# Seven large work tiles, five gate tiles, three cells and two attention tiles in the second stage of a four-layer graph network

## The chip, the cores and the metric

The kernel runs on one core of one Trainium2 chip. The metric is the device time of one execution in microseconds (us), lower is better, given as the median of several runs of the same program.

The core has a matrix engine (TensorE, "PE" in the profile, with its weight loads listed apart as "PEld"), a vector engine (VectorE, "DVE"), an activation engine (ScalarE, "ACT"), a general one (GpSimd, "POOL") and one that issues DMAs here (SyncE, "SP"). Each has its own instruction queue and works it off in order; they meet at semaphores. Matrix products land in PSUM, a memory of eight banks. Everything else lives in SBUF, 128 partitions wide.

## What is computed

The input `x` has 128 samples of 64 nodes with 256 features, and `adj` is one 64x64 adjacency matrix. Four layers follow each other, each with a residual sum and a layer norm:

```
x = layernorm(x + L0(x, adj))   # three graph convolutions, 256 -> 512 -> 1024 -> 256
x = layernorm(x + L1(x, adj))   # U relu(U^T x W1 + b1) W2 + b2, U the eigenvectors of the Laplacian
x = layernorm(x + L2(x, adj))   # two graph convolutions, then windowed LSTMs
x = layernorm(x + L3(x, adj))   # attention of the nodes, masked by adj
```

The LSTM part of L2 is the heavy one. For p = 1, 2, 3, 4 the nodes are cut into windows of p in a row, a small LSTM with its own weights runs over each window, and its last state replaces the last node of the window:

```
for p in range(1, 5):
    wins = h[:, :nw * p, :].reshape(Bv * nw, p, Hd)
    last = _lstm_last(Wih[p - 1], Whh[p - 1], bih[p - 1], bhh[p - 1], wins)
    h = h.at[:, idx, :].set(last.reshape(Bv, nw, Hd))
```

so the LSTM of p+1 reads what that of p wrote, and each LSTM step needs the state of the step before.

## The kernel before

The 8192 rows (128 samples x 64 nodes) are 64 tiles of 128 rows, worked on in 16 groups of 4 tiles. All arithmetic is float32.

**First stage** (lines up to about 1120, 0 to about 795 us): layer 0 for all groups, with the eigenvectors of the Laplacian worked out in between on DVE. Its matmuls are issued in `mm` (line 940). It isn't touched by the change.

**Second stage** (from about 797 us to the end): layers 1 to 3. `unit` (line 1518) describes the work of one unit. Groups 0 to 11 go in six units of two groups, groups 12 to 15 in four units of one. For each group a unit calls `layer1`, then `to_lstm` (the two graph convolutions, then `lstm` for p = 1, 2, 3); then for the pair together `four` (the LSTM of p = 4, whose later steps go through `halves`, a product scheme with fewer multiplications that needs sums of the weights, "sums"); then for each group `from_lstm` (back to rows, residual sum, norm) and `layer3` (attention, residual sum, norm, output DMA). The text calls the passage in which a unit runs `from_lstm` and `layer3` a changeover, because by then another unit has to supply the LSTM matmuls.

`norm` (line 1232) is a chain across engines: DVE takes statistics, POOL adds a constant and raises to the power -1/2, DVE (or ACT in the last groups) scales the rows `X`. Matmuls that read the new `X` wait for that chain.

The order of the instructions isn't written by hand. A planner, `Plan` (lines 104 to 233), first notes each operation with an estimated length and its dependencies (`note`), then emits them one by one (`run`). It keeps up to `UNITS` = 3 units open at a time. At each pick it takes, for each engine, the operations that are ready, works out when each could begin by its own estimates, and emits the earliest, an operation of an older group first where they tie. All its instructions pass through `emit`, so the profile shows them all under line 156.

Buffers enter the planner as counted slots. An operation that opens a new tile can begin only once a slot of that kind is free; if all are held, it is no candidate and something else is taken. A slot comes free when the last operation that touches its tile is done. The kinds are:

| kind | what it holds | size per partition | slots before | name, line |
|---|---|---|---|---|
| `w` | large work tiles: results of `mixed`, the LSTM input and output `hT`, the differences in `halves`, `xT`, `hT` and `hn` of `layer3` | 4 KB | 6 | `WIDE`, 742 |
| `gates` | the gates of one half of an LSTM step | 4 KB | 6 | `GATES`, 743 |
| `att` | exponentials of the scores in `layer3` | 2 KB | 3 | `ATT`, 744 |
| `c` | LSTM cell states | 2 KB | 4 | `CELLS`, 745 |
| `hs` | LSTM outputs between steps | 2 KB | 4 | `OUTS`, 746 |
| `v` | small work tiles | 2 KB | 4 | in the call of `Plan` |
| `ps` | PSUM banks | | 8 | in the call of `Plan` |

The `hT` of a group is a `w` tile that is opened in `to_lstm` and held until `from_lstm` has read it. An `lstm` step opens two `gates` tiles; an LSTM with p > 1 opens one cell tile for all its steps. The four names reach the planner in one call:

```
plan = Plan({...}, place,
            {"ps": 8, "w": WIDE, "v": 4, "gates": GATES, "c": CELLS, "hs": OUTS, "att": ATT, ...})
```

`ATT` is also the length of the loop that allocates the attention tiles and clears each of them with a memset on POOL (line 1149). While more than three groups are left, a guard in `candidates` also keeps younger units from taking the last free slots of a kind: it leaves the oldest unit as many as `MOST` says, 4 of `w`, 2 of `v`, `ps` banks 4, 2 of `gates`, 2 of `hs`, and one of each other kind, less those that the oldest unit holds already.

Of the kernel before, what the change touches and what calls it, by code (L numbers as in the profile page):

```python
# [738 lines left out]
EPS = 1e-5  # L739
UNITS = 3  # L740
ENDING = (14, 15)
WIDE = 6
GATES = 6
ATT = 3
CELLS = 4
OUTS = 4
LASTS = 3
SINGLE = 4
# [59 lines left out]
def kernel(  # L808
# [337 lines left out]
    att = []  # L1146
    for i in range(ATT):
        att.append(wb.tile([P, 4, P], F32, name=f"att{i}"))
# [3 lines left out]
    def place(tag, slot, shape):  # L1152
# [4 lines left out]
        if tag in ("w", "v", "gates", "c", "hs"):  # L1157
# [3 lines left out]
    plan = Plan({"PE": nc.tensor, "DVE": nc.vector, "ACT": nc.scalar, "POOL": nc.gpsimd, "SP": nc.sync}, place,  # L1161
                {"ps": 8, "w": WIDE, "v": 4, "gates": GATES, "c": CELLS, "hs": OUTS, "att": ATT, "mx": 4, "sm": 4, "st": 4, "mv": 4,
                 "rs": 4, "nm": 4})
# [434 lines left out]
```

## Time and profile before

| | |
|---|---|
| median of 3 runs | 2471.87 us (2471.45 to 2472.79) |
| the profiled execution's own time | 2474.36 us |
| its span, first to last instruction | 2472.6 us |
| mean granted clock of PE | 0.996 |
| PE busy | 2438.2 us (99%), 15500 matmul records |
| DVE busy | 1618.9 us (65%) |
| ACT busy | 1072.3 us (43%) |
| POOL busy | 137.4 us (6%) |

Engine times are sums over the span. Each float32 matmul of the program leaves two matmul records, a transpose one. A row of the profile reads: line, engine, operation, the tile written, an arrow, the tiles read, shapes, count. In a list of waits, "PE ps <- DVE X" means that PE was about to write a `ps` tile and was released by the DVE instruction that wrote `X`. In a table of stretches each row is one stretch of the span: its limits and length, the busy time of each engine with its instruction count, then the share of full clock that PE was granted, the share of the DMA engines and their rate in GB/s.

### The profile page before, as it was taken

The numbers are of one execution on the slowest core, as the hardware profiler recorded it, in microseconds if no ns is written. First come the engines' busy times: TensorE is split into PE (matmuls) and PEld (weight loads), VectorE is DVE, ScalarE is ACT, GpSimd is POOL, SyncE is SP. The second block draws the span as 40 slices with busy tenths as digits, with TensorE's granted clock in tenths as the row PEclk, the third lists the DMA queues.
The fourth block names the chain that finished last, engine by engine and source line by source line (L and its number), as shares of the span: only waits on it lengthen the run. The fifth ranks groups of instructions, "written<-read, shape, count | busy, mean of one in ns | idle before, by whom it ended". The sixth has DMA issues, their size and how long they took to land.

```text
span 2472.6 us, 40811 instructions
## 1 busy us (share of the span) xinstructions
PE 2438.2 (99%) x15500; PEld 2162.5 (87%) x15500; DVE 1618.9 (65%) x5676; ACT 1072.3 (43%) x2610; POOL 137.4 (6%) x316
## 2 busy tenths in 40 slices
PE   9999999999999999999999999999999999999997
PEld 7788888878887899989978999999998997988996
DVE  6888787778887274583674476476458468374336
ACT  2343343333333354444434444444444444445555
POOL 0000000000000010010010000000001001010002
PEclk9999999999999999999999999999999999999999
DMA  6000000000000110010000001001001000000000
GB/s 225 9 1 18 10 9 10 9 10 9 10 1 1 64 56 1 1 35 1 1 18 18 1 1 35 1 1 35 1 1 35 1 1 18 1 10 1 1 1 27
DMA packets 27973, 42.69 MB, mean 17 GB/s; under 512 B 2945, under 2 KB 22145, under 8 KB 27777
## 3 DMA queue, kind: packets, MB, share of 16 engines
q1 hardware_dynamic: 27424, 39.81, 4.6%
q8 instruction: 122, 2.00, 0.3%
q14 instruction: 75, 0.61, 0.1%
q10 hardware_dynamic: 352, 0.28, 0.0%
HBM read 26.45 MB, written 13.63 MB: 16 GB/s over the span
## 4 chain that ended last, share of the span: by engine, by line
PE 93%; DVE 5%; POOL 1%; DMA 1%; ACT 0%; issue 0%; SPq 0%; ACTq 0%; POOLq 0%; DVEq 0%
PE ps L156 61%; PE ps L940 31%; DVE X L156 1%; DVE D L52 1%; DVE st L156 1%; PE pc L296 1%; DMA XA<-in_x_dram 1%; DVE gates L156 0%; POOL rs L156 0%; DVE tw L52 0%; DVE w L156 0%; ACT gates L156 0%; DVE h L52 0%; DVE u L52 0%; DVE mv L156 0%
## 5 line engine op out<-in xcount | busy, mean ns | idle before, releaser
L156 PE MATMUL ps<-w,wih 128*128 128x168 f32 (+2 forms) x4144 | 753.7, 315 | 0.9 <-DVE gates L156 0.9
L156 PEld LDWEIGHTS ps<-w,wih 128*128 128x128 f32 x4144 | 647.6, 191 | 38.1 <-issue 6.9
L156 ACT ACTIVATE gates<-ps,cbi 128x168 f32<-128x168 f32 (+2 forms) x832 | 342.8, 418 | 368.5 <-PE ps L156 360.3
L156 PE MATMUL ps<-hs,whh 128*128 128x168 f32 (+1 forms) x1952 | 344.8, 291 | 0.0
L156 PEld LDWEIGHTS ps<-hs,whh 128*128 128x128 f32 x1952 | 289.2, 191 | 1.7 <-issue 1.4
L156 PE MATMUL ps<-w,sums 128*128 128x128 f32 x1776 | 237.1, 275 | 0.0
L156 DVE SCALAR_TENSOR_TENSOR gates<-gates 128x256 f32<-128x256 f32 (+2 forms) x220 | 84.0, 382 | 222.8 <-ACT gates L156 222.2
L940 PE MATMUL ps<-aw,h 128*128 128x256 f32 x1024 | 227.2, 379 | 0.0
L156 PEld LDWEIGHTS ps<-w,sums 128*128 128x128 f32 x1776 | 217.5, 192 | 0.6 <-issue 0.5
L940 PEld LDWEIGHTS ps<-aw,h 128*128 128x128 f32 x1024 | 192.9, 190 | 25.9 <-ACT h L949 0.5
L156 ACT ACTIVATE gates<-gates,cbi 128x256 f32<-128x256 f32 x272 | 116.4, 497 | 206.6 <-DVE gates L156 206.5
L949 ACT ACTIVATE h<-h 128x512 f32<-128x512 f32 x128 | 80.5, 630 | 196.6 <-DVE h L52 196.5
L156 DVE TENSOR_TENSOR gates<-gates,ps 128x256 f32<-128x256 f32 x340 | 128.7, 417 | 21.3 <-PE ps L156 15.9
L940 PE MATMUL ps<-ss,tw 128*128 128x256 f32 x512 | 117.9, 380 | 0.0
L940 PE MATMUL ps<-ss,aw 128*128 128x256 f32 x512 | 117.3, 379 | 0.0
L940 PE MATMUL ps<-m,aw 128*128 128x256 f32 x512 | 117.1, 380 | 0.0
L156 DVE SCALAR_TENSOR_TENSOR c<-gates,c 128x256 f32<-128x256 f32 (+2 forms) x156 | 57.2, 367 | 88.6 <-ACT gates L156 88.2
L940 PE MATMUL ps<-aw,m 128*128 128x512 f32 x256 | 114.8, 594 | 0.1
L940 PEld LDWEIGHTS ps<-ss,aw 128*128 128x128 f32 x512 | 96.6, 190 | 12.8
L940 PEld LDWEIGHTS ps<-ss,tw 128*128 128x128 f32 x512 | 96.3, 190 | 12.9 <-issue 0.2
L156 DVE TENSOR_TENSOR gates<-v,ps 128x256 f32<-128x256 f32 x136 | 55.5, 417 | 79.5 <-ACT v L156 47.7
L940 PEld LDWEIGHTS ps<-m,aw 128*128 128x128 f32 x512 | 95.6, 190 | 12.6 <-issue 0.5
(314 smaller groups left out, 3743.0 us busy)
## 6 DMA issues: line engine op xcount, KB each, us to landing
out_dram<-X SPq DMA_DIRECT2D x64, 128.0 KB, 1.7
rest<-XA SPq DMA_DIRECT2D x10, 512.0 KB, 2.6
X<-rest SPq DMA_DIRECT2D x10, 512.0 KB, 3.2
XA<-in_x_dram SPq DMA_DIRECT2D x18, 256.0 KB, 6.2
wih<-in_c_ih_dram SPq DMA_DIRECT2D x4, 1024.0 KB, 7.4
aw<-in_a_w_dram SPq DMA_DIRECT2D x3, 1024.0 KB, 10.8
X<-in_x_dram SPq DMA_DIRECT2D x12, 256.0 KB, 5.9
whh<-in_c_hh_dram SPq DMA_DIRECT2D x3, 1024.0 KB, 9.3
```

Of the source, the lines that this page charges most:

```text
L52: return getattr(self.engine, name)(out, *args, **kw)
L156: getattr(e, name)(*[real(x) for x in args], **{k: real(v) for k, v in kw.items()})
L296: PE.matmul(out, lhsT, rhs, start=True, stop=True)
L940: PE.matmul(out, lhsT, rhs, start=start, stop=stop)
L949: S.activation(dst, src, AF.Relu)
```

## The change

Four constants take other values. Nothing else in the file differs.

```diff
-WIDE = 6
-GATES = 6
-ATT = 3
-CELLS = 4
+WIDE = 7
+GATES = 5
+ATT = 2
+CELLS = 3
 OUTS = 4
 LASTS = 3
```

The tiles of these four kinds take 7 x 4 + 5 x 4 + 2 x 2 + 3 x 2 = 58 KB of each partition instead of 6 x 4 + 6 x 4 + 3 x 2 + 4 x 2 = 62 KB. The planner gets other slot counts, so it may emit the second stage in another order; one memset of an attention tile falls away.

## The prediction

> **What bounds the kernel now.** I read the page first, then stretches of the second stage by busy time of each engine, then the waits of the tensor engine in the worst stretch, then the chain that ended last and the timeline there. The page gives each engine's busy time, share and instructions:
>
> ```profile
> span 2472.6 us, 40811 instructions
> PE 2438.2 (99%) x15500; PEld 2162.5 (87%) x15500; DVE 1618.9 (65%) x5676; ACT 1072.3 (43%) x2610; POOL 137.4 (6%) x316
> ```
>
> PE is idle for 2472.6 - 2438.2 = 34.4 us. A change that leaves the matmuls alone can only win from that, and from matmuls that run slowly. The stretches show where it lies (columns: length, busy PE, its weight loads PEld, DVE, ACT, POOL, then PE's granted clock):
>
> ```profile
> core 0: us, PE busy (x) PEld busy (x) DVE busy (x) ACT busy (x) POOL busy (x), PEclk, DMA share, GB/s
> 1160.00:1310.00 150.00, 142.94 (x1044) 129.44 (x1043) 101.01 (x303) 60.26 (x138) 13.50 (x28) 0.98 0.05 15
> 1310.00:1465.00 155.00, 155.00 (x1114) 147.12 (x1113) 78.49 (x225) 73.81 (x185) 0.00 (x0) 1.00 0.00 1
> 1520.00:1880.00 360.00, 359.94 (x2582) 331.96 (x2581) 221.24 (x646) 170.01 (x405) 18.92 (x40) 1.00 0.02 7
> 2030.00:2110.00 80.00, 76.35 (x531) 65.23 (x530) 61.90 (x181) 36.16 (x76) 9.70 (x20) 1.00 0.04 14
> 2420.00:2472.60 52.60, 36.87 (x286) 29.72 (x284) 36.74 (x125) 25.16 (x61) 15.07 (x40) 0.88 0.09 31
> ```
>
> Length less busy PE: 7.06, 0, 0.06, 3.65 and 15.73 us. So the stage has two holes, around 1280 and 2050, and a tail. Both holes are **changeovers**: the oldest unit leaves the LSTM and runs from_lstm, layer3 and two norms, while the next unit should supply LSTM matmuls. In the first hole PE waits for (us in total, times, longest):
>
> ```profile
> PE ps L156 <- DVE X L156: 4.4, 2, 3.6
> PE ps L156 <- DVE gates L156: 0.9, 1, 0.9
> PE ps L156 <- ACT att L156: 0.8, 1, 0.8
> PE ps L156 <- DVE w L156: 0.8, 1, 0.8
> ```
>
> X is written by the norm. The timeline there, and in the changeover at 1680 that costs nothing:
>
> ```profile
> 1298.08 0.61 PE L156 MATMUL ps<-adT,w 128*128 128x128 f32 x4
> 1302.32 1.29 PE L156 MATMUL ps<-adT,X 128*128 128x128 f32 x8 [3.64 <-DVE X L156]
> ...
> 1678.61 1.03 PE L156 MATMUL ps<-w,wih 128*128 128x256 f32 x4
> 1683.40 2.75 PE L156 MATMUL ps<-w,wih 128*128 128x256 f32 x12
> ```
>
> At 1298 nothing is left but matmuls that need a normalized X; between 1678 and 1686 gate matmuls (w,wih) of the next unit stand between the same steps. A hole costs twice, since PE then runs at about half clock:
>
> ```profile
> 1268.80:1272.50 3.70, 3.65 (x5) 1.59 (x6) 3.67 (x13) 0.02 (x1) 1.84 (x4) 0.54 0.00 0
> 1302.30:1306.50 4.20, 4.18 (x16) 3.56 (x17) 2.22 (x5) 1.58 (x4) 0.77 (x2) 0.61 0.37 125
> ```
>
> Lost: 3.70 x 0.46 + 4.20 x 0.39 = 3.3 us, which counts as busy.
>
> **What the Trainium skill says.** "Perfetto Trace Analysis", Optimization Strategy: bubbles that repeat on the engine that should be saturated can mean too little SBUF for the next tile. The trace agrees in that both holes lie at the same step. The same page, Identifying the Most-Contended Engine, warns that busy PE is no measure of headroom; agreed, as the 3.3 us above hide in it. "TensorE: Matmul & The Clock Gate", What's actually happening, has the clock halve after an idle window of about 3.4 us. After the 3.64 us hole the clock was 0.61, which fits; at 1268.8 it was 0.54 though the holes before were only 0.8 us each, so here a half-idle window was enough.
>
> **The change part by part.**
>
> *Work.* All four numbers are counts of buffers. Every matmul, VectorE, ScalarE and SyncE instruction stays, in number and shape; only one 128x512 memset of an attention tile goes (0.52 us on POOL at 845, for which nobody waits: nothing). The DMA order on SyncE is the same. POOL keeps its order apart from that memset. So the gain is idle time and clock alone.
>
> *Where the order moves.* The planner emits by which buffers are free, so the order of PE, DVE and ACT changes. Comparing the two orders: PE's is the same up to the matmul at 1068.0 us and again from 2321.0 us to the end (DVE's and ACT's to 1016 and from 2293 and 2319). Hence stage one and the tail (15.73 us idle) stay: nothing. Between them lie 1253.0 us with 1240.38 busy, so **12.62 us idle plus 3.3 us of slow clock: at most 15.9 us** can be won.
>
> *Seven large work tiles.* A unit of two groups holds a "w" tile per group from to_lstm to from_lstm, and others for a few steps. With six, none is free at 10.3% of the planner's picks; with seven at 4.5%. Before, during the last step of four of groups 2 and 3, the count is 0 to 2 and to_lstm of the next pair goes in drips, so at 1261 its LSTM has not begun. The LSTM matmuls that stand among the from_lstm and layer3 steps of each pair, counted in the orders (a full changeover has about 30 us of PE work):
>
> | changeover at, us | LSTM matmuls before | PE idle before, us | LSTM matmuls after |
> |---|---|---|---|
> | 1062 | 24 | 0.0 | 24 |
> | 1261 | 0 | 6.14, and 3.3 of clock | 18 |
> | 1472 | 14 | 0.45 | 16 |
> | 1657 | 24 | 0.06 | 20 |
> | 1859 | 20 | 0.64 | 20 |
> | 2046 | 12 | 3.65 | 20 |
> | 2164 | 34 | 0.35 | 34 |
>
> Outside the table, 0.92 us is a gates wait at 1181 and 0.38 one at 1975. The idle column is from the stretches and sums, with these two, to 12.6. In the trace of before, a changeover with 14 or more costs 0 to 0.64 us, with 12 or fewer 3.65 to 9.4. So I price the second at 0.3 (saving 6.14 + 3.3 - 0.3 = 9.1) and the sixth at 0.2 (saving 3.4). I leave 0.45, 0.06 and 0.64 about as they are, and the 0.92: the same neighbours (a transform by ut, then a gate matmul whose bank is still being read) stand together one pair later. The small waits near 1975 and 2193 may go; I take half of 0.73, 0.4. Sum: 9.1 + 3.4 + 0.4 = **12.9 us**.
>
> *Five gate tiles, three cells, two attention tiles.* Before, none of these is ever used up. After, gates are all taken at 1.2% of the picks, cells at 7.3%, attention at 0.4%. A step that waits for one isn't placed, so nothing queues behind it on its engine and PE takes another unit's matmuls. The cost is cover: an LSTM step of the younger unit starts later. Cover in the order is 16 to 34 matmuls, so I take 0. Bounds: if one middle changeover loses its cover, 9.4 us as at 1261; on the good side nothing beyond the 15.9.
>
> *What is late next.* In the second changeover DVE is 32.97 us busy of 40.4 (1262 to 1302.4); in the fourth, which has no hole, 27.46 of 33.5. DVE comes next, but has room in a stretch of this length once PE's LSTM work sits in it.
>
> The sum is against the profiled execution: span 2472.6 - 12.9 = 2459.7, its own time 2474.36 - 12.9 = 2461.5. The median of the runs is 2.49 lower than that time: 2471.87 - 12.9 = **2459.0 us**.
>
> **Rivals.** About 0.2%, 4.9 us, is what a measurement of this kernel can tell from no change.
>
> 1. *Cover without effect: DVE sets the changeover.* The norm chain (add, statistics, POOL's power, scale) is mostly DVE, and the new LSTM steps bring DVE work into it. For it: in the second hole DVE was busy while PE waited, 82% of the whole changeover. Against it: the fourth has the same 82% and no idle. If half of the two holes stays, the gain is 12.5/2 = 6.2; if a third of it is left, 4. I put this case at 2467, between 2465 and 2471.
>
> 2. *Cells become the bound: slower.* With three, the younger unit's second window length can't start before the oldest unit releases a cell in its last step, just before the changeover, so that the cover is missing where it is needed. Price: 9.4 us for each bare changeover, as at 1261. Today's two holes together cost 13.1, of which 12.5 would go, so it decides from the second bare one (18.8 - 12.5 = +6.3). With three of the five middle ones, 28.2 - 12.5 = +15.7: 2487. Against it: the counts in the table.
>
> 3. *The change does nothing.* It would need the planner never to use the seventh tile. The differing order speaks against it; it leaves 2471.9.
>
> **How the numbers follow.** Forecast 0.80; the first rival 0.12, half of it beyond 0.2%; the second 0.05; the third 0.03. Faster by over 0.2%: 0.80 + 0.05 = 0.85. Same: 0.06 + 0.03 = 0.09. Slower: 0.05, and 0.01 for orders that neither covers: 0.06. Low end: 15.9 us won and up to 3 us of short starts behind holes, 2453. High end: 2467, the middle of the first rival. Outside remain half of that rival and the others, near 2 in 10.
>
> **What would show it.** Right: between 1160 and 1310 PE idle under 1.6 us and the clock at 1.00; in 2030 to 2110 under 1 us; gate matmuls (w,wih) between the dw and att matmuls of the second changeover; idle from there to 2320 under 4 us; the last 150 us as before. Wrong: a PE wait of over 2 us for X, w or gates in any changeover, or ACT or DVE waits that end just ahead of an LSTM matmul in the middle of an LSTM stretch, which would be cells or gates.

## The result, and the profile after

The changed kernel takes 2457.62 us (median of 5 runs, 2457.22 to 2459.16), the one before 2471.56 (5 runs, 2470.68 to 2472.79). The ratio is 0.9941, 95% interval 0.993 to 0.9952: 13.9 us faster, where 12.9 was forecast. The page of the changed kernel:

```profile
span 2455.8 us, 40814 instructions
PE 2431.6 (99%) x15500; PEld 2158.3 (88%) x15500; DVE 1618.6 (66%) x5676; ACT 1073.0 (44%) x2610; POOL 137.5 (6%) x315
```

The matmul count is the same; PE is busy 6.6 us less with the same work, and idle for 24.2 us instead of 34.4. The same stretches as before, and the last 52.6 us (columns as there):

```profile
1160.00:1310.00 150.00, 149.56 (x1128) 138.05 (x1128) 108.32 (x321) 66.58 (x156) 11.88 (x24) 1.00 0.05 15
1310.00:1465.00 155.00, 154.07 (x1131) 147.05 (x1130) 90.33 (x269) 70.86 (x174) 6.94 (x14) 1.00 0.00 1
1520.00:1880.00 360.00, 359.91 (x2613) 332.75 (x2612) 222.77 (x656) 171.27 (x411) 20.40 (x40) 1.00 0.03 8
2030.00:2110.00 80.00, 79.63 (x576) 71.34 (x575) 61.50 (x186) 36.83 (x87) 9.54 (x20) 1.00 0.04 14
2403.20:2455.80 52.60, 36.92 (x300) 29.88 (x298) 37.30 (x128) 26.47 (x64) 15.00 (x40) 0.91 0.09 31
```

PE's idle time in them is 0.44, 0.93, 0.09, 0.37 and 15.68 us: both holes are closed and the tail is as it was. Between 861 and 2320 us, the stretch with every changeover of a pair, all that PE waits for is now:

```profile
PE ps L156 <- DVE w L156: 1.0, 3, 0.4
PE ps L156 <- DVE gates L156: 0.9, 1, 0.9
```

No wait for X is left. The timeline of the second changeover shows why. Gate matmuls of the next unit stand between the attention's transposes (att), the products with it (w,v) and the first matmuls on a normalized X:

```profile
1279.34 4.48 PE L156 MATMUL ps<-w,wih 128*128 128x256 f32 x20
1283.66 0.60 PE L156 MATMUL ps<-ident,att 128*128 128x128 f32 x4
1284.09 1.03 PE L156 MATMUL ps<-w,wih 128*128 128x256 f32 x4
1284.96 1.97 PE L156 MATMUL ps<-w,v 128*128 128x256 f32 x8
1286.76 2.75 PE L156 MATMUL ps<-w,wih 128*128 128x256 f32 x12
1289.35 1.95 PE L156 MATMUL ps<-adT,X 128*128 128x128 f32 x16
```

**Where the time came from.** I cut the two profiled executions at the first layer 1 matmul (861 us in both) and at the program's 597th matmul from the end, from which on the PE order is the same. In between, PE idle falls from 12.62 to 2.15 us (-10.5) and PE busy from 1447.54 to 1442.70 (-4.8). Of these 4.8 us, 3.4 are clock: before, two stretches of 3.41 us (from 1269.07 and from 1303.21 us) ran at half clock, after, none does. The remaining 1.4 I put down to slower first matmuls after holes; I did not take them apart. From the cut to the last matmul it is 138.27 and 136.76 us (-1.5, with the same idle time): before has one more half-clock stretch there, from 2429.61 us. The order there is unchanged, so this part is a difference between two executions and no gain of the change. The sum is -16.8, the difference of the spans. The medians differ by 13.9, since the profiled execution of before (2474.36) was 2.8 us above its median and that of after is its median.

### The profile page after: what moved, and what is told of

The parts are those of the page before. It is cut to its first block, busy times and chain, and to the rows that moved or that the text cites. A ratio compares the mean times of both kernels' runs of the same rounds, so it can differ in the third digit from the quotient of the medians.

```text
span 2455.8 us, 40814 instructions
## 1 busy us (share of the span) xinstructions
PE 2431.6 (99%) x15500; PEld 2158.3 (88%) x15500; DVE 1618.6 (66%) x5676; ACT 1073.0 (44%) x2610; POOL 137.5 (6%) x315
## 4 chain that ended last, share of the span: by engine, by line
PE 94%; DVE 4%; DMA 1%; ACT 0%; issue 0%; POOL 0%; SPq 0%; ACTq 0%; POOLq 0%; DVEq 0%
PE ps L156 62%; PE ps L940 31%; DVE D L52 1%; DVE X L156 1%; PE pc L296 1%; DMA XA<-in_x_dram 1%; DVE st L156 0%; DVE tw L52 0%; POOL rs L156 0%; DVE w L156 0%; DVE h L52 0%; ACT gates L156 0%; DVE gates L156 0%; DVE u L52 0%; DVE v L156 0%
## 5 line engine op out<-in xcount | busy, mean ns | idle before, releaser
L156 PE MATMUL ps<-w,wih 128*128 128x128 f32 (+2 forms) x4144 | 752.7, 315 | 0.9 <-DVE gates L156 0.9
L940 PEld LDWEIGHTS ps<-ss,tw 128*128 128x128 f32 x512 | 96.3, 190 | 12.9 <-issue 0.2
```

The lines of the kernel that those rows point to most:

```text
L156: getattr(e, name)(*[real(x) for x in args], **{k: real(v) for k, v in kw.items()})
L940: PE.matmul(out, lhsT, rhs, start=start, stop=stop)
```

## The experiments

Theory A is that of the prediction: the seventh "w" tile lets the next unit's LSTM start early enough to supply cover. Its rivals are that the three reductions make the better order, that the tile itself counts and not the cover, and that VectorE sets the length of a changeover. Ratios are to the kernel before, run on the same chip; the medians of the latter were 2472.07, 2472.55 and 2472.38 us in the three batches (experiments 1 to 4, 5 to 8, 9 to 12), on three chips. The changed kernel was not run again beside them, so a difference from its 2457.62 us compares two batches and can be off by about 1 us. The edits are given in short form.

**1. The reductions alone.**

```diff
-GATES, ATT, CELLS = 6, 3, 4
+GATES, ATT, CELLS = 5, 2, 3      # WIDE stays 6
```

> Six large work tiles, five gate tiles, three cells, two attention tiles: the three reductions without the seventh large tile. Theory A (the seventh large tile lets the next unit's LSTM start before the changeover and supplies cover): its order has 24, 0, 14, 24, 20, 12, 34 LSTM matmuls in the seven changeovers, the same as before the change, so 2471.6 us within 2, with idle of about 7 us between 1160 and 1310 us and 3.7 us between 2030 and 2110. Theory B (the smaller counts hold younger units back and so make the better order): near 2458 us. Theory C (a smaller count is a cost that the seventh tile outweighs): over 2474 us.

Measured: 2472.24 us, ratio 1.000 (0.9992 to 1.0008). The stretches are those of before:

```profile
1160.00:1310.00 150.00, 142.92 (x1044) 129.39 (x1043) 100.93 (x303) 60.17 (x138) 13.46 (x28) 0.98 0.05 15
2030.00:2110.00 80.00, 76.38 (x531) 65.26 (x530) 61.65 (x180) 36.03 (x75) 9.68 (x20) 1.00 0.04 14
```

In its trace PE and VectorE run the same instructions in exactly the same order as in the trace of before. So the reductions neither bring the gain nor cost anything (the interval reaches 0.08% each way). What they bring is room: the four kinds would take 66 KB per partition with seven large tiles and the other counts as before, a combination that was not run.

**2. Seven large tiles with five gate tiles, the rest as before.**

```diff
-WIDE, GATES = 6, 6
+WIDE, GATES = 7, 5      # ATT 3, CELLS 4
```

> Seven large work tiles and five gate tiles, attention tiles and cells as before (three and four). Theory A: the changeovers have 24, 18, 16, 20, 20, 20, 34 LSTM matmuls, as in the changed kernel, so 2457.6 us within 1.5. Theory C (cells at three, all taken at 7.3% of the picks, cost something): 2 us or more below the changed kernel, 2455 or less. Theory B (fewer cells and attention tiles are part of the gain): 2460 or more.

Measured: 2457.43 us, ratio 0.9939 (0.9926 to 0.9951), the changed kernel within 0.2 us, and with PE's instructions in exactly its order. So cells and attention tiles at three and two cost nothing that shows, though cells are all taken at 7.3% of the picks.

**3. Five large tiles.**

```diff
-WIDE = 6
+WIDE = 5
```

> Five large work tiles, all else as before the change: the dose in the other direction. Theory A: the changeovers have 0, 0, 10, 0, 0, 24, 22 LSTM matmuls. Four bare ones at about 9.4 us each and one with 10 at about 3.7 give 41.3, in place of the 9.4 + 3.7 = 13.1 of before the change, so about 28 us more than before: 2500, between 2485 and 2525. If large tiles are also missing inside the LSTM stretches, more than that. Theory D (VectorE alone sets the length of a changeover, cover or not): within 5 us of 2471.6.

Measured: 2544.05 us, ratio 1.0289 (1.0274 to 1.0303): 72 us more, where 28 was expected, and outside the range of 2485 to 2525. The direction speaks for A and against VectorE, but the price was too low. The changeover near 1900, and the one near 2130, which has 24 LSTM matmuls:

```profile
1880.00:1960.00 80.00, 65.14 (x393) 51.57 (x394) 51.91 (x146) 27.54 (x56) 9.53 (x20) 0.89 0.08 27
2110.00:2160.00 50.00, 45.00 (x274) 34.38 (x272) 41.66 (x128) 23.20 (x47) 9.55 (x20) 0.97 0.07 22
```

In the first, PE is idle for 14.9 us, and 14.2 us of its work ran at half clock (in 1896.49 to 1910.14 and 1927.21 to 1930.62), which costs 7.1: 22 us for one bare changeover. Added up in the same way, the other three without LSTM matmuls cost 13 (1060 to 1100 us), 9 (1260 to 1310) and 17 (1660 to 1730). The cheap one has 28 matmuls of other kinds, from younger units, between its steps in the order; the other three have none. The changeover at 1261 in the kernel before, priced at 9.4, was a mild case of this sort, with 32 such matmuls. So these matmuls cover too, only less well. And 24 LSTM matmuls did not close the changeover near 2130: PE is idle for 5.0 us in and around it. A further 4.4 us of idle lie in an LSTM stretch (1760 to 1880).

**4. Eight large tiles.**

```diff
-WIDE = 7
+WIDE = 8      # GATES 5, ATT 2, CELLS 3
```

> Eight large work tiles, the other three counts as in the changed kernel. Theory A: every changeover has 14 or more LSTM matmuls (24, 16, 16, 24, 16, 24, 14), so there is nothing left to win in them: 2457.6 within 3, rather above than below, since in its order some gate matmuls near 1790 us follow closely on the VectorE steps that they need (up to 4 us of it bare: 2461). Theory E (more large tiles win further, as the count of none free falls from 4.5% to 3.8% of the picks): 2455 or less.

Measured: 2463.08 us, ratio 0.9961 (0.9949 to 0.9974), 5.5 us slower than with seven, so theory E falls; it is also above the 2461 that A allowed. The interval of its ratio just overlaps that of the changed kernel, but experiment 2, on the same chip and with the changed kernel's order, ran from 2456.83 to 2458.81 us and this one from 2461.26 to 2464.81. Most of it is one new hole outside any changeover, near the place that was named, where nothing but an LSTM step is left and its input (w, written by VectorE) is late:

```profile
1774.34 0.45 PE L156 MATMUL ps<-w,wih 128*128 128x168 f32 x2
1777.48 3.98 PE L156 MATMUL ps<-w,wih 128*128 128x168 f32 x16 [2.70 <-DVE w L156]
```

The hole is 2.70 us, and the 3.41 us from 1778.41 ran at half clock, another 1.7. More tiles don't win further: with one more the order shifts, and another place goes bare.

**5. Six tiles, with cover all the same.** The guard in `candidates` reserves four large tiles for the oldest unit.

```diff
-    MOST = {"w": 4, "v": 2, ...}
+    MOST = {"w": 2, "v": 2, ...}      # the kernel before otherwise
```

> The kernel before with its six large work tiles, six gate tiles, four cells and three attention tiles; only the guard's reserve of large tiles for the oldest unit is 2 in place of 4, so that a younger unit may take one of the last tiles. Theory A' (it is the cover that counts, and the seventh tile only makes it possible): LSTM matmuls per changeover in its order 24, 24, 24, 20, 20, 20, 34, so the holes of 7 and 3.7 us are gone and the time is that of the changed kernel, 2457.6, within 3, although no seventh tile exists. Theory F (the tile itself is what counts, through fewer waits for a slot): within 4 of 2471.6.

Measured: 2458.01 us, ratio 0.9943 (0.9931 to 0.9956), as the changed kernel, without a seventh tile:

```profile
1160.00:1310.00 150.00, 147.78 (x1104) 135.84 (x1103) 104.24 (x314) 65.87 (x154) 11.64 (x24) 1.00 0.05 15
2030.00:2110.00 80.00, 79.63 (x577) 71.36 (x576) 61.55 (x186) 36.85 (x86) 9.74 (x20) 1.00 0.04 14
```

Idle: 2.22 us (0.92 of it the gates wait, 1.29 in the second changeover, which has 24 LSTM matmuls) and 0.37.

**6. Seven tiles, with the cover taken away.**

```diff
-    MOST = {"w": 4, "v": 2, ...}
+    MOST = {"w": 5, "v": 2, ...}      # the changed kernel otherwise
```

> The changed kernel with its seven, five, three and two tiles; only the guard's reserve of large tiles for the oldest unit is 5 in place of 4. Theory A': LSTM matmuls per changeover 24, 0, 20, 0, 20, 22, 26, so two bare ones. With five large tiles a bare changeover cost 17 to 24 us (idle and clock), before the change 9.4. So 2457.6 plus 2 times 9.4 to 24: between 2475 and 2505, near 2490, slower than before the change although there are seven tiles. Theory F: within 4 of 2457.6.

Measured: 2493.9 us, ratio 1.009 (1.0076 to 1.0104): 36.3 us slower than the changed kernel with the same tiles. Its second changeover:

```profile
1250.00:1304.00 54.00, 39.86 (x248) 29.78 (x247) 38.90 (x114) 16.26 (x33) 7.70 (x16) 0.87 0.12 38
```

That is 14.1 us idle and 12.7 us of work at half clock, worth 6.4: 20.5 us. The other changeover without LSTM matmuls (1660 to 1712) cost only 7.7; that one has 34 matmuls of other kinds in it, the one shown has none. Experiments 5 and 6 together settle it between tile and order: the gain comes without the tile and goes with the tile in place, according to what stands in the changeovers. The tile counts as far as it lets the next unit go ahead, and the guard on the six tiles was another way to the same gain.

**7 and 8. Less VectorE work, before and after.**

```diff
-        V.tensor_scalar(z, s, 0.0, -1e16, op0=ALU.is_equal, op1=ALU.mult)
-        V.tensor_add(s, s, z)      # planned as before, not emitted
```

> The kernel before without two VectorE steps of the attention's mask (the test for a score of zero and the addition of the large negative number are left out), the order of all that remains unchanged. That is 36 instructions of 0.27 and 0.42 us, 12.3 us of VectorE work, of which 1.4 in each pair's changeover. Theory A with VectorE as pace of a bare changeover only: the two holes shrink by up to 1.4 us each and by some of the slow clock, the tail by up to 1.4: 1 to 5 us less, 2466.5 to 2470.5. Theory D (VectorE sets the length of every changeover): 6 us or more less.

> The changed kernel without the same two VectorE steps of the attention's mask, the order of all that remains unchanged. Theory A: the covered changeovers don't feel VectorE, only the tail may, by up to 1.4 us: 2456 to 2457.6, and the middle of the second stage unchanged within 0.7 us. Theory D: 1.4 us in each of six changeovers, 2449 to 2452.

Measured: 2472.29 us on the kernel before (ratio 0.9999, 0.9991 to 1.0007) and 2456.73 on the changed one, 0.9 below it. Taking 12.3 us off VectorE wins nothing clear in either; the rival that the amount of VectorE work sets every changeover (6 us or more) falls. My own expectation for the first, 1 to 5 us, was not borne out either: 0.3 us, with an interval that allows at most 2.2. The trace says why:

```profile
1291.77 0.66 PE L156 MATMUL ps<-ident,att 128*128 128x128 f32 x4 [0.36 <-ACT att L156]
1299.57 0.60 PE L156 MATMUL ps<-adT,X 128*128 128x128 f32 x3 [3.64 <-DVE X L156]
```

The hole at the attention shrank from 0.85 to 0.36 us, the large one behind it stayed at 3.64: it begins with the product that the norm needs, and runs through adding, statistics, POOL's power and scaling, none of which I had shortened. Whether a shorter norm chain would shrink a bare changeover was not tried; in the covered ones of the changed kernel PE has no wait for X that it could shorten.

**9 and 10. Gates and attention tiles down by one more.**

```diff
-GATES = 5
+GATES = 4      # 9; the changed kernel otherwise
-ATT = 2
+ATT = 1        # 10; the changed kernel otherwise
```

> The changed kernel with four gate tiles in place of five (all taken at 4.9% of the planner's picks, after 1.2%). Cover in the changeovers of its order: 24, 18, 18, 18, 24, 16, 26 LSTM matmuls, none bare. Theory G (cover alone decides): 2457.6 within 2. Theory H (once gates are short, what follows a changeover is uncovered too, since a younger LSTM step waits for the older one's gates; in its order several gate and row matmuls follow closely on VectorE and ScalarE steps, 1 to 2 us each in about six places): 2463 to 2470.

> The changed kernel with one attention tile in place of two (taken at 3.0% of the picks, after 0.4%). Theory A: the cover is the same (24, 18, 16, 20, 20, 20, 34), so the middle is unchanged; only the tail, in which four attention blocks lie close together, may wait for the tile: 0 to 3.5 us more, 2457.6 to 2461. If attention tiles were what the rival of few tiles is about, over 2465.

Measured: 2467.82 us (ratio 0.9982, 0.9975 to 0.9989) and 2460.01 (0.995, 0.9933 to 0.9967), so 10.2 and 2.4 us slower than the changed kernel. Theory G falls, H is met; for the 2.4 us the intervals of the two ratios overlap, but the trace has a wait for it. For four gate tiles, PE between 861 and 2320 us waits for:

```profile
PE ps L156 <- ACT w L156: 6.4, 5, 1.6
PE ps L156 <- DVE w L156: 5.6, 7, 1.9
PE ps L156 <- ACT att L156: 0.2, 1, 0.2
```

The first two lines are twelve holes of 0.2 to 1.9 us. Seven of them, 8.9 us in all, lie just before or within the first 10 us of changeovers that have 16 to 24 LSTM matmuls. So the count of cover isn't enough; where it stands counts too. With one attention tile only the tail grew (a wait of 2.3 us for att).

**11 and 12. The tail.**

```diff
-ENDING = (14, 15)
+ENDING = (13, 14, 15)      # 11; the changed kernel otherwise
+ENDING = (15,)             # 12; the changed kernel otherwise
```

> The changed kernel with three last groups instead of two whose norms go to ScalarE and whose attention is split in two halves. It aims at the tail (15.7 us of idle PE in the last 52.6 us, VectorE busy 37.3 of them). If VectorE paces the tail, moving one more group's scaling to ScalarE (four scalings of 0.41 us twice) helps by 1 to 3 us: 2455 to 2457. If the chain through POOL and ScalarE paces it: 2458 to 2461.

> The changed kernel with one last group instead of two that ends on ScalarE and in halves. The opposite step: if VectorE paces the tail 2459 to 2463; if the chain through POOL and ScalarE does, 2454 to 2457.

Measured: 2467.84 us (ratio 0.9981, 0.9974 to 0.9988) and 2454.64 (ratio 0.9928, 0.9914 to 0.9943). The second beats both kernels, by 3.0 us under the changed one: its four runs all lie below the changed kernel's five, though the intervals of the two ratios overlap. The first lies well above both of its readings. PE's waits in the tail of the changed kernel (from 2390 us), and in the last version, in this order:

```profile
PE ps L156 <- ACT X L156: 1.3, 3, 0.9
PE ps L156 <- ACT att L156: 0.5, 1, 0.5
PE ps L156 <- ACT w L156: 0.3, 1, 0.3
PE ps L156 <- ACT v L156: 0.2, 1, 0.2
```

```profile
PE ps L156 <- ACT v L156: 0.7, 1, 0.7
```

With three endings the waits for ACT X and ACT att are 4.3 and 6.6 us. So ScalarE comes last in the waits of the tail, and the time falls when fewer groups end on it. That is the direction of the second reading; its size for three endings, at most 2461, was missed by 7 us. Which part does it is open: the constant moves the scaling to ScalarE and also splits the attention in two, and I didn't try these apart.

## Why the prediction was right, point by point

- *Bound.* "At most 15.9 us can be won", idle plus clock, from the stretch where the order moves. Measured there, in one execution each: 10.5 + 4.8 = 15.3, with 2.15 us of idle left. So about 17.4 was there to be won: the 3.3 us of clock was right (3.4), but the busy time also held 1.4 us that the bound did not count.
- *Second changeover, 9.1 us.* Right. The stretch from 1160 to 1310 has 0.44 us of idle, with the 0.92 us wait moved out of it, and clock 1.00; 0.3 was left for the changeover.
- *Sixth, 3.4 us.* Right: 3.65 became 0.37, and 0.2 was left for it.
- *"Both holes lie at the same step".* Only the changeover is of the same kind. Around 2050 there is no wait for X; 2.05 of the 3.65 us is a wait of the next unit's own graph convolution (adT,w), just before the oldest unit's first transposes:

```profile
2045.66 1.16 PE L156 MATMUL ps<-adT,w 128*128 128x128 f32 x8 [2.05 <-ACT w L156]
```

- *The 0.92 us gates wait moves to the next pair.* Right: it stands at 1377, with 0.92 us.
- *The 0.45, 0.06 and 0.64 "about as they are".* Too cautious. The stretches 1465 to 1520, 1520 to 1880 and 1880 to 1920 now have 0.00, 0.09 and 0.00 us; 1.06 us more was won than the sum held.
- *Reductions at no cost.* Right, and shown by experiments 1 and 2 with intervals of about 0.1%. That PE simply takes another unit's matmuls when a gate tile is missing holds for five gates, not for four (10.2 us).
- *Tail unchanged.* In idle time yes (15.73 and 15.68); the half-clock stretch there, which makes the 1.5 us, was in one execution and not in the other.
- *The sum.* The mechanism is right, but that 12.9 meets 13.9 so closely is in part luck. Between the two profiled executions the span fell by 16.8 us, 3.9 more than forecast: 0.9 of idle, 1.5 of busy time in the middle, 1.5 of clock in the tail. To come from the profiled execution to the median, the forecast took 2.5 us off for both kernels; the changed kernel's profiled execution turned out to be its median, and that took back most of the 3.9.
- *"A hole costs twice".* Not every one: the hole of 2.05 us at 2045.7 and the two behind it were followed by full clock.
- *Rival 2.* The case did not come up. Its price was mis-sized: "9.4 us for each bare changeover" was taken from one mild case. Experiments 3 and 6 give 8 and 9 us where some 30 other matmuls stand in the changeover, 13 to 22 us where none do. One of the latter would have outweighed the 12.5 us.
- *The rule "14 or more costs 0 to 0.64".* It held for the changed kernel and not in general: experiment 3 idles 5.0 us at a changeover with 24, and experiment 9 has holes of 1.47 us at the start of two with 18.

## What to carry to other kernels

When one engine is 99% busy, look for the stretches in which it is not, and for another stretch of the same kind in the same trace that has no hole: what stands between the same steps there is the lever. A buffer count that lets the next unit begin early is worth the cover it brings and no more, where cover is any matmul that does not wait for the chain; a slot rule can bring the same cover without the buffer (experiment 5), and another buffer can move the hole elsewhere (experiment 4). Compare the order of the instructions before and after, and price each place where it differs from a place like it.

## What the runs showed of the hardware

The slow clock behind a hole is not a fixed price, and the traces show what it hangs on. In all 14 profiles the granted clock is 1.00 or 0.50 and nothing else. Where a profile has more than one slow stretch (nine do), they begin whole multiples of 3.41 us apart, and those that end while PE works last 3.41 us or a multiple. So the clock is set in steps of 3.41 us, and where the steps lie against the program differs from execution to execution. Here is the place around 1268 us, cut at these steps, in the kernel before and in the version of it with less VectorE work. Both have two holes of 0.80 and 0.81 us:

```profile
1265.65:1269.07 3.42, 1.75 (x10) 1.02 (x10) 3.35 (x11) 0.59 (x1) 1.07 (x3) 1.00 0.00 0
1269.07:1272.48 3.41, 3.41 (x5) 1.35 (x5) 3.38 (x11) 0.00 (x0) 1.81 (x4) 0.50 0.00 0
```

```profile
1263.18:1266.60 3.42, 2.62 (x17) 1.87 (x16) 3.35 (x13) 1.10 (x3) 2.00 (x4) 1.00 0.00 0
1266.60:1270.01 3.41, 2.56 (x9) 1.27 (x9) 3.41 (x13) 0.58 (x1) 0.92 (x2) 1.00 0.00 0
1270.01:1273.42 3.41, 3.41 (x19) 1.93 (x19) 2.52 (x9) 1.38 (x2) 1.60 (x4) 1.00 0.00 0
```

Before, both holes fell into one step, PE was busy for 1.75 us of it, and the next step ran at half clock. In the other version they fell into two steps with 2.62 and 2.56 us busy, and nothing slowed down. Over all 14 profiles from 861 us on, each of the 22 full-clock steps with at most 1.50 us of busy PE was followed by half clock, none of the more than 6400 with 2.04 us or more was, and of the 16 between these, 8 were. A slow step full of work costs 1.7 us.

The spread of the runs goes with the clock. Of the 72 runs of the kernel before beside the experiments, the 19 above 2473 us all have a mean clock of 0.996, the 42 of up to 2472.6 us all 0.997. That it is the steps behind its holes that come and go is likely, but was not traced run by run. Five runs of either kernel spread alike, by 2.1 us before and 1.9 after.
